# Loading 68 rows of one x block in sixteen 17-row transfers from GpSimd's queue

## The chip, the cores and the metric

One core of one Trainium2 chip. The metric is the time of one execution on the device, in microseconds (us), lower is better.

## The reference, cut to what matters

```python
# inputs (4096, 32, 64) f32, W (496, 64, 64) f32, out (4096, 496, 64) f32
idx_i, idx_j = np.triu_indices(32, k=1)          # 496 pairs i < j
vidots = jnp.einsum('bpd,pde->bpe', inputs[:, idx_i, :], W)
return vidots * inputs[:, idx_j, :]
```

The input is 33.5 MB, the weights 8.1 MB, and the output 520 MB: the kernel's work on memory is nearly all output.

## The kernel before

The 4,096 rows are 16 blocks of 256; a block holds two rows on each of 128 partitions and is computed in two passes of 46 steps. A pass `t` has five groups of steps, and each group fills one buffer `ot` and sends it out as one transfer of 2.9 to 3.4 MB. In a step TensorE multiplies into PSUM, then VectorE multiplies the result by x into `ot`; in seven steps of a pass ("aside") ACT copies PSUM to SBUF and GpSimd makes the product.

```python
xpool = ctx.enter_context(tc.tile_pool(name="xpool", bufs=2))   # x blocks
tpool = ctx.enter_context(tc.tile_pool(name="tpool", bufs=4))
opool = ctx.enter_context(tc.tile_pool(name="opool", bufs=3))   # outputs
# ... (cut)
def new_x(blk):
    xs[blk] = xpool.tile([P, 1 + NB * F, D], F32, tag="xs", name=f"xs_{blk}")
    nc.gpsimd.memset(xs[blk][:, 0, :], 0.0)

def load_x(blk, eng, k0=0, k1=NB):
    src = rows_of(x, blk).rearrange("(p k) f d -> p (k f) d", k=NB)
    eng.dma_start(out=xs[blk][:, 1 + k0 * F : 1 + k1 * F, :], in_=src[:, k0 * F : k1 * F, :])
# ... (cut)
LATE = 6
loads = {place[blk * NB, LATE]: blk + 1 for blk in range(2, NBLK - 1)}
# ... (cut) in the loop over the steps:
    if s in loads:
        new_x(loads[s])
        load_x(loads[s], nc.scalar)          # 128 rows of 16 KB, 2 MB
# ... (cut)
    if i in aside and c0 == 0 and s not in no_aside:
        nc.scalar.copy(tmp, src)
        nc.gpsimd.tensor_mul(dst, tmp, xj)
    else:
        nc.vector.tensor_mul(dst, src, xj)
    if pa + m in ends:
        nc.sync.dma_start(out=..., in_=ot[...])   # one output
```

## Time and profile before

| | before |
|---|---|
| time, median of 2 | 1354.19 us (1353.6 to 1354.78) |
| DMA engines, mean busy | 90% or more in 39 of 40 slices |
| TensorE / VectorE / GpSimd busy | 87% / 71% / 39% |
| output transfers | 161, 520 MB |
| loads of x by ACT's queue | 14 of 2 MB |

The prediction below shows the page's lines for this.

### The profile page before, as it was taken

The numbers are of one execution on the slowest core, as the hardware profiler recorded it, in microseconds if no ns is written. First come the engines' busy times: TensorE is split into PE (matmuls) and PEld (weight loads), VectorE is DVE, ScalarE is ACT, GpSimd is POOL, SyncE is SP. The second block draws the span as 40 slices with busy tenths as digits, with TensorE's granted clock in tenths as the row PEclk, the third lists the DMA queues.
The fourth block names the chain that finished last, engine by engine and source line by source line (L and its number), as shares of the span: only waits on it lengthen the run. The fifth ranks groups of instructions, "written<-read, shape, count | busy, mean of one in ns | idle before, by whom it ended". The sixth has DMA issues, their size and how long they took to land.

```text
span 1353.3 us, 17856 instructions
## 1 busy us (share of the span) xinstructions
PE 1180.3 (87%) x7424; PEld 690.9 (51%) x7424; DVE 956.9 (71%) x1262; ACT 374.1 (28%) x367; POOL 530.2 (39%) x246
## 2 busy tenths in 40 slices
PE   6989889889799897988879989888987989988994
PEld 4556545545455454555445545454554545545552
DVE  5778768767677676776757777676775767767774
ACT  3432222222232232222222222222222222223221
POOL 1813424444243443433444334433434434344431
PEclk9989999989999898999989999899998999989997
DMA  9999999999999999999999999999999999999997
GB/s 386 370 426 408 424 427 431 428 432 431 418 414 419 433 412 418 422 413 426 428 407 422 417 425 410 423 421 407 425 410 426 419 422 427 401 432 428 415 417 319
DMA packets 26273, 562.92 MB, mean 416 GB/s; under 512 B 2912, under 2 KB 2912, under 8 KB 3040
## 3 DMA queue, kind: packets, MB, share of 16 engines
q1 hardware_dynamic: 24048, 530.59, 92.4%
q10 hardware_dynamic: 2144, 31.20, 5.5%
q8 instruction: 58, 0.95, 0.3%
q14 instruction: 23, 0.19, 0.0%
HBM read 41.68 MB, written 520.09 MB: 415 GB/s over the span
## 4 chain that ended last, share of the span: by engine, by line
DMA 50%; PE 25%; DVE 17%; POOL 3%; issue 2%; ACT 0%; DVEq 0%; SPq 0%; POOLq 0%; ACTq 0%
DMA out_dram<-ot 50%; PE ps L211 20%; DVE ot L228 17%; PE ptx L114 4%; POOL ot L226 3%; PE ptw L104 1%; DMA raw<-in_L_rec_W_dram 1%; ACT tmp L225 0%; DVE rp L95 0%; POOL rp L95 0%; DVEq L228 0%; ACT wT L107 0%; SPq L76 0%; POOLq L226 0%; SPq L233 0%
## 5 line engine op out<-in xcount | busy, mean ns | idle before, releaser
L228 DVE TENSOR_TENSOR ot<-ps,xs 128x1024 f32<-128x1024 f32 (+15 forms) x1252 | 945.6, 808 | 364.7 <-DMA out_dram<-ot 185.9
L211 PE MATMUL ps<-wT,xT 64*128 64x512 f32 (+13 forms) x6272 | 1034.9, 473 | 132.8 <-DVE ot L228 121.3
L211 PEld LDWEIGHTS ps<-wT,xT 64*128 64x128 f32 x6272 | 563.7, 197 | 569.9 <-DVE ot L228 306.8
L226 POOL TENSOR_TENSOR ot<-tmp,xs 128x1024 f32<-128x1024 f32 x220 | 519.6, 2362 | 647.4 <-ACT tmp L225 457.1
L225 ACT COPY tmp<-ps 128x1024 f32<-128x1024 f32 x220 | 222.7, 1012 | 500.1 <-PE ps L211 459.6
L118 ACT COPY xT<-ptx 128x1024 f32<-128x1024 f32 x128 | 129.6, 1012 | 428.2 <-PE ptx L114 428.2
L114 PE MATMUL ptx<-ident,xs 128*128 128x128 f32 x1024 | 141.2, 281 | 18.5 <-DVE ot L228 9.9
L114 PEld LDWEIGHTS ptx<-ident,xs 128*128 128x128 f32 x1024 | 111.0, 142 | 64.3 <-issue 44.1
L72 POOL MEMSET xs<- 128x64 f32 x16 | 2.4, 152 | 148.6 <-DVE ot L228 148.6
L104 PE MATMUL ptw<-ident,rp 128*128 128x128 f32 (+1 forms) x128 | 19.2, 305 | 3.9 <-DVE rp L95 3.9
L104 PEld LDWEIGHTS ptw<-ident,rp 128*128 128x128 f32 (+1 forms) x128 | 16.2, 160 | 10.3 <-DVE rp L95 5.0
L107 ACT COPY wT<-ptw 128x1024 f32<-128x1024 f32 (+1 forms) x15 | 14.8, 984 | 21.4 <-PE ptw L104 21.4
L95 DVE COPY rp<-raw 128x1024 f32<-128x1024 f32 (+1 forms) x9 | 10.7, 1219 | 11.1 <-DMA raw<-in_L_rec_W_dram 11.1
L95 POOL COPY rp<-raw 128x1024 f32<-128x1024 f32 x4 | 8.0, 1994 | 0.1
L95 ACT COPY rp<-raw 112x1024 f32<-112x1024 f32 (+1 forms) x3 | 5.9, 1959 | 5.1 <-POOL ot L226 3.3
L107 DVE COPY wT<-ptw 128x1024 f32<-128x1024 f32 x1 | 1.2, 1224 | 3.3 <-PE ptw L104 3.3
L118 ACT ACT_TABLE_LOAD x1 | 1.3, 1283 | 0.7 <-PEq L251 0.7
masks.py:197 POOL MEMSET ident<- 128x128 f32 x1 | 0.2, 206 | 0.3 <-POOLq L251 0.3
masks.py:199 POOL TENSOR_SCALAR_AFFINE_SELECT ident<-ident 128x128 f32<-128x128 f32 x1 | 0.3, 295 | 0.0
L251 POOL MEMSET const-float32-0.0<- 128x1 f32 x1 | 0.1, 99 | 0.2 <-issue 0.2
L251 POOL MEMSET const-bfloat16-1.0<- 128x1 bf16 x1 | 0.1, 102 | 0.0
L251 POOL MEMSET const-uint8-127<- 128x1 uint8 x1 | 0.1, 102 | 0.0
(1 smaller groups left out, 0.1 us busy)
## 6 DMA issues: line engine op xcount, KB each, us to landing
out_dram<-ot SPq DMA_DIRECT2D x64, 3360.0 KB, 16.2
out_dram<-ot SPq DMA_DIRECT2D x32, 3168.0 KB, 15.4
out_dram<-ot SPq DMA_DIRECT2D x32, 3104.0 KB, 17.0
out_dram<-ot SPq DMA_DIRECT2D x31, 2880.0 KB, 16.4
xs<-in_r_inputs_dram ACTq DMA_DIRECT2D x14, 2048.0 KB, 16.6
raw<-in_L_rec_W_dram SPq DMA_DIRECT2D x3, 2048.0 KB, 14.3
xs<-in_r_inputs_dram SPq DMA_DIRECT2D x2, 1024.0 KB, 10.9
xs<-in_r_inputs_dram SPq DMA_DIRECT2D x1, 2048.0 KB, 24.6
```

Source lines behind the costliest of these rows:

```text
L72: nc.gpsimd.memset(xs[blk][:, 0, :], 0.0)
L95: copy(rp[:r], src[:, k * EU : (k + 1) * EU])
L104: nc.tensor.transpose(pt[:, n, :r], rp[:r, n].rearrange("p h d -> p (h d)"), ident[:r, :r])
L107: copy(wT[c][:, :, k * EU : (k + 1) * EU], pt[:, :, :r].rearrange("p e r -> p r e"))
L114: nc.tensor.transpose(pt[:, n, :], xs[blk][:, s : s + 2, :].rearrange("p f d -> p (f d)"), ident)
L118: copy(xT, pt)
L211: nc.tensor.matmul(ps[:, h, lo - pa : hi - pa, :], xT[blk, kt, n // RUN][h * D : (h + 1) * D, n % RUN, :], wT[c][h * D : (h + 1) * D, lo - ...
L225: nc.scalar.copy(tmp, src)
L226: nc.gpsimd.tensor_mul(dst, tmp, xj)
L228: nc.vector.tensor_mul(dst, src, xj)
L251: nc = _bacc.Bacc("TRN2", target_bir_lowering=False, num_devices=1)
```

## The change

The intent: take one x block of sixteen (block 7) mostly off ACT's queue and load it little by little from GpSimd's queue while block 6 is computed. 68 rows go in 16 pieces, four groups of 17 rows times four quarters of the 32 fields, written as one piece every fourth step; the other 60 rows stay with ACT's queue. The bytes are the same.

```diff
-    def load_x(blk: int, eng, k0: int = 0, k1: int = NB):
+    def load_x(blk: int, eng, k0: int = 0, k1: int = NB, r0: int = 0):
         src = rows_of(x, blk).rearrange("(p k) f d -> p (k f) d", k=NB)
-        eng.dma_start(out=xs[blk][:, 1 + k0 * F : 1 + k1 * F, :], in_=src[:, k0 * F : k1 * F, :])
+        eng.dma_start(
+            out=xs[blk][r0:, 1 + k0 * F : 1 + k1 * F, :], in_=src[r0:, k0 * F : k1 * F, :]
+        )
+    ODD, ODDR, ODDQ = 7, 17, 4
+
+    def load_piece(blk: int, n: int):
+        r, q = divmod(n, ODDQ)
+        rows = slice(r * ODDR, (r + 1) * ODDR)
+        cut = slice(q * F // ODDQ, (q + 1) * F // ODDQ)
+        src = rows_of(x, blk).rearrange("(p k) f d -> p k f d", k=NB)
+        dst = xs[blk][:, 1:, :].rearrange("p (k f) d -> p k f d", k=NB)
+        nc.gpsimd.dma_start(out=dst[rows, :, cut, :], in_=src[rows, :, cut, :])
 # ... (cut)
+    pieces = {place[(ODD - 1) * NB, LATE] + 4 * n + 1: n for n in range(ODDQ * ODDQ)}
 # ... (cut)
-            load_x(loads[s], nc.scalar)
+            load_x(loads[s], nc.scalar, r0=ODDR * ODDQ if loads[s] == ODD else 0)
+        if s in pieces:
+            load_piece(ODD, pieces[s])
```

## The prediction

The record as it stood before the result. What it took from no trace or run of this case is cut, and the cuts are marked. Its sum came to +7 us for the stall (5.5 + 1.5), and with the other outcomes weighed in to 1358.5 us. Terms of that sum are cut: what an issue on GpSimd takes, which the sums below still count as 1 us (an assumption then; the changed kernel's trace shows 0.972 us, mean of 16), and the time from an output's issue to its first byte, which is the step from 542.5 to 544.5 and from 552.5 to 554 (not shown before the result; 0.83 us measured in it). Cut, too, are the terms for how many bytes the late engine would be spared or given, which is why the hidden form has a range of 1350 to 1357.

> **What bounds the kernel now.** I read the page's rows by slice first, then the DMA queues, the groups, the waits, and the trace around the place where block 7 is loaded.
>
> ```profile
> DMA  9999999999999999999999999999999999999997
> ...
> DMA packets 26273, 562.92 MB, mean 416 GB/s; under 512 B 2912, under 2 KB 2912, under 8 KB 3040
> ...
> q1 hardware_dynamic: 24048, 530.59, 92.4%
> q10 hardware_dynamic: 2144, 31.20, 5.5%
> q8 instruction: 58, 0.95, 0.3%
> ...
> DMA 50%; PE 25%; DVE 17%; POOL 3%; issue 2%; ACT 0%; DVEq 0%; SPq 0%; POOLq 0%; ACTq 0%
> ...
> L228 DVE TENSOR_TENSOR ot<-ps,xs 128x1024 f32<-128x1024 f32 (+15 forms) x1252 | 945.6, 808 | 364.7 <-DMA out_dram<-ot 185.9
> ...
> out_dram<-ot SPq DMA_DIRECT2D x64, 3360.0 KB, 16.2
> ...
> xs<-in_r_inputs_dram ACTq DMA_DIRECT2D x14, 2048.0 KB, 16.6
> ```
>
> The DMA engines are at 90% or more in every slice but the last; no compute engine is. The chain that ended last is half DMA, all of it output. VectorE's largest idle time ends with the landing of an earlier output (three ot buffers). A 3,360 KB output needs 16.2 us to land though 16 engines move it in about 8: two outputs are normally queued.
>
> The trace's semaphore events show more. Each transfer ends with 16 increments, one per DMA engine. Times of issue, of the median engine and of the last one, around block 7's load, in us:
>
> ```
> output t=11 g=3   issued 505.39  median 514.89  last 523.23
> output t=11 g=4   issued 514.33  median 529.15  last 534.36
> x, block 7 (ACT)  issued 514.37  median 529.33  last 531.39
> output t=12 g=0   issued 520.65  median 535.97  last 541.35
> output t=12 g=1   issued 529.08  median 543.32  last 549.02
> output t=12 g=2   issued 541.76  median 550.88  last 556.84
> ```
>
> One engine ends 5 to 8 us after the others, at every output. At the kernel's end it moves packets until 1351.2 when the others stopped at 1345.0. A 26,880-byte packet takes 996 ns, so an average engine's 35.1 MB need 35.1/0.02699 = about 1,302 us; the late one has about 40 us more work. The 58 instruction packets (one per 22 us, 16 KB, 0.9 us each, some 50 us) are of that size; that they are its extra load is my inference. **The bound is the queue of this late engine**; the others have 3% to spare. It idles only if an output is issued later than its previous one ends: output g=0 of t=12 came at 520.65 and that engine could begin it at 534, so a delay under about 8 to 13 us is hidden.
>
> [...] during block 7's load one engine's packets run q10 16 KB, q1 26 KB, q10 16 KB, q1 26 KB and so on, singly, 8 of each; the load took 17.02 us for 2 MB.
> [...]
>
> **The change, part by part.**
> *Bytes.* The same 2 MB. 16,384 bytes take 611 ns and 8,192 take 309, so a packet costs 7 ns plus its bytes at 27.1 per ns, and 2 KB cost 83 ns. 16 pieces x 34 packets = 544 packets instead of 68 of 16 KB: 476 x 7 ns / 16 engines = 0.2 us. [...]
>
> *GpSimd's work.* [...]
>
> ```profile
> 514.42 0.15 POOL L72 MEMSET xs<- 128x64 f32 x1 [10.22 <-DVE ot L228]
> 517.82 2.36 POOL L226 TENSOR_TENSOR ot<-tmp,xs 128x1024 f32<-128x1024 f32 x1 [3.25 <-ACT tmp L225]
> 523.36 2.36 POOL L226 TENSOR_TENSOR ot<-tmp,xs 128x1024 f32<-128x1024 f32 x1 [3.18 <-DMA out_dram<-ot]
> 526.68 2.37 POOL L226 TENSOR_TENSOR ot<-tmp,xs 128x1024 f32<-128x1024 f32 x1 [0.96 <-ACT tmp L225]
> 534.49 2.35 POOL L226 TENSOR_TENSOR ot<-tmp,xs 128x1024 f32<-128x1024 f32 x1 [5.44 <-issue]
> 539.37 2.36 POOL L226 TENSOR_TENSOR ot<-tmp,xs 128x1024 f32<-128x1024 f32 x1 [2.53 <-ACT tmp L225]
> ```
>
> This is GpSimd in before, from the memset of block 7's buffer on. The instruction order of the built changed kernel is not one issue every fourth step: five pieces follow the memset directly, then the product that before ran at 517.82, two pieces, the product of 523.36, one piece, and then pieces 8, 9 and 10 ahead of the product of 526.68; 11, 12, 13 ahead of the next; 14 and 15 ahead of the one after. GpSimd's transfers share eight semaphores, so **piece n from 8 on waits in GpSimd's stream for piece n−8 to have landed**, with the products behind it. TensorE's and VectorE's order is unchanged; their new waits are for pieces needed from about 593 us on.
>
> *When piece 0 lands.* On one engine, taking turns with output packets, its 17 turns of 4 KB take 17 x (1.0 + 0.16) = 20 us; with 34 turns of 2 KB, 34 x 1.08 = 37 us. Issued at about 515.5, it lands at 537 in the first case. In the second it lands there too, since while GpSimd waits no output is issued, and an ordinary engine has no output left from about 534 on; the rest then passes at 83 ns a packet.
>
> *What that costs.* GpSimd would want to issue piece 8 at about 527 (five pieces to 519.6, product to 522, two pieces, product to 526.5, one piece). Waiting to 537, plus three issues and the product of 2.37 us, puts output t=12 g=1 at 542.5 instead of 529.08. The late engine ends t=12 g=0 at 541.35 − 2.4 us (64 KB of x not yet moved) = 539. [...] it idles 539 to 544.5: 5.5 us. Three more issues, a product, two issues, a product (3 + 2.4 + 2 + 2.4 = 10 us) put output g=2 at 552.5, at the engine about 554, where g=1 ends at 552.5: 1.5 us more. After that GpSimd has only products and catches up. Sum: **+7 us**, once, since only one of sixteen blocks is so loaded. Pieces 8 to 15 go out by 551 and have 40 us before use; no second stall.
>
> **Rivals.**
> *Hidden anyway.* If a piece is spread over nine engines (4 packets each, about 6 us to land), or its 34 descriptors go as one packet in one turn (about 3 us), piece 8 never waits. The issues then put output g=1 at 533 instead of 529, within the slack. Cost 0[...]. [...] Time 1350 to 1357.
> *All pieces on one engine.* [...] 544 packets x 83 ns = 45 us fall on one engine within a block, of which 8 to 14 us are hidden by queued outputs: +30 to +37 us, 1385 to 1392. [...] It is the main way to over 2%.
> *GpSimd becomes the bound.* If an issue costs 3 us instead of 1, five ahead of the first product delay output g=0 by 12 us, just about the slack, and the later ones add up: +10 to +15 us. [...]
>
> **Range and chances.** I give the 7 us stall one half, the hidden form (mean 0) 0.35, the expensive forms 0.15 (mean +22): 3.5 + 0 + 3.3 = about +6.8; the most likely single outcomes lie between 0 and +7, so I put it below the mean, at 1358.5. Range 1352 to 1371. Over 2% slower means above 1381: 0.07. Over 2% faster would need 27 us saved at an engine that keeps its bytes: 0.01. Within 2%: 0.92.
>
> **What would show it.** Right: an idle GpSimd of about 10 us ahead of a piece in block 6, ended by the landing of an earlier GpSimd load; output t=12 g=1 issued some 13 us later than before; a dip in the DMA row in one slice near 540 us; landings of pieces of 20 us and more; 544 packets of 2 KB; VectorE not waiting for x. Wrong if pieces land in under 10 us (the stall vanishes), if GpSimd's products lie far apart without a landing between them (the issue is dear), or if one engine's output lags by tens of us [...]. A change of VectorE's or TensorE's busy time is not expected.

## More of the kernel before

One more view serves for comparison: the view by windows, which gives for a stretch of time each engine's busy time (with the number of instructions), then the granted clock of TensorE, the share that the DMA engines were busy, and GB/s. This is the kernel before, in the stretch where the changed kernel will differ:

```profile
core 0: us, PE busy (x) PEld busy (x) DVE busy (x) ACT busy (x) POOL busy (x), PEclk, DMA share, GB/s
535.00:545.00 10.00, 9.70 (x58) 6.42 (x60) 6.61 (x11) 3.26 (x4) 6.57 (x3) 0.79 1.01 432
```

The last two figures are to be seen: the engines are full (1.01) and move 432 GB/s.

## The result

The changed kernel takes 1362.62 us (1362.52 to 1362.72, 2 runs) against 1354.19: 8.4 us more. Ratios here and below are the mean time of one kernel's fast runs over that of the other's of the same rounds, so not quite the ratio of the medians quoted; here 1.006, with a 95% interval of 1.0036 to 1.0084. That is within 2%, and inside the predicted range.

The page of the changed kernel: DMA share and GB/s by slice, packets, queues, and the group of GpSimd's new issues (busy time, mean ns of one, idle time before them and what ended it).

```profile
DMA  9999999999999997999999999999999999999997
GB/s 381 371 432 420 422 428 432 424 432 424 419 424 415 410 432 290 384 422 431 428 429 430 425 425 427 421 421 413 426 412 420 421 418 421 413 435 417 418 420 317
DMA packets 30813, 562.97 MB, mean 414 GB/s; under 512 B 7247, under 2 KB 7247, under 8 KB 7647
...
q0 software_dynamic: 4608, 1.15, 0.5%
...
L90 POOL DMA_DIRECT2D xs<-in_r_inputs_dram x16 | 15.5, 972 | 12.8 <-DMA xs<-in_r_inputs_dram 12.2
```

The DMA row now has one 7, in slice 16 (510 to 544 us), where GB/s fall to 290, and to 384 in the next. GpSimd waited 12.2 us ahead of its own issues, until an earlier load of x had landed. The new queue q0 carried 4,608 packets, though the 1.11 MB of x that it moves fill only 272 of 4 KB: the trace's packet records show 272 of 4,096 bytes, 256 of 4 (the increments) and **4,080 of 8 bytes**.

GpSimd's instructions in order of time (start, duration, instruction, count; in brackets the idle time before it and what ended it):

```profile
514.08 0.15 POOL L72 MEMSET xs<- 128x64 f32 x1 [10.37 <-DVE ot L245]
514.78 4.92 POOL L90 DMA_DIRECT2D xs<-in_r_inputs_dram  x5 [0.55 <-issue]
519.73 2.35 POOL L243 TENSOR_TENSOR ot<-tmp,xs 128x1024 f32<-128x1024 f32 x1
522.02 1.93 POOL L90 DMA_DIRECT2D xs<-in_r_inputs_dram  x2
524.05 2.34 POOL L243 TENSOR_TENSOR ot<-tmp,xs 128x1024 f32<-128x1024 f32 x1
526.35 0.98 POOL L90 DMA_DIRECT2D xs<-in_r_inputs_dram  x1
538.45 0.96 POOL L90 DMA_DIRECT2D xs<-in_r_inputs_dram  x1 [11.12 <-DMA xs<-in_r_inputs_dram]
540.51 1.91 POOL L90 DMA_DIRECT2D xs<-in_r_inputs_dram  x2 [1.10 <-DMA xs<-in_r_inputs_dram]
542.44 2.37 POOL L243 TENSOR_TENSOR ot<-tmp,xs 128x1024 f32<-128x1024 f32 x1
544.74 2.88 POOL L90 DMA_DIRECT2D xs<-in_r_inputs_dram  x3
```

Pieces 0 to 7 go out until 527.3. Piece 8 then waits 11.12 us for piece 0 to land, piece 9 waits again, and the product that ran at 526.68 before stands behind them until 542.44. The chain of waits of the changed kernel passes through just this:

```profile
515.88 24.34 DMA xs<-in_r_inputs_dram
...
540.51 1.91 POOL xs L90 x2
542.44 2.09 POOL ot L243
```

The stretch that was full before, by windows:

```profile
535.00:545.00 10.00, 8.48 (x61) 4.67 (x58) 6.15 (x10) 3.20 (x4) 5.43 (x5) 1.00 0.32 74
```

The DMA engines are busy 0.32 of it and move 74 GB/s instead of 432. The issues and last landings of the outputs, from the trace's semaphore events (us; last = the sixteenth increment):

```
                    before              after
                 issued   last      issued   last      last, later by
t=12 group 0     520.65  541.35     522.11  540.03       -1.3
t=12 group 1     529.08  549.02     544.84  555.97        7.0
t=12 group 2     541.76  556.84     554.27  567.81       11.0
t=12 group 3     549.42  565.11     558.87  575.79       10.7
t=13 group 3     587.88  606.49     598.17  615.37        8.9
```

Output group 1 is issued 15.8 us later. The late engine's last packet of group 0 ended at 539.47, and the first packets of group 1 are at 545.67: a hole of 6.2 us, in which, but for one packet of instructions, only pieces moved. Group 2 ends 11 us later than before; at the end of the program 7.4 us of that are left (spans 1360.7 and 1353.3 us).

### The profile page after: what moved, and what is told of

Its sections match the earlier page's. It is cut to its first block, busy times and chain, and to the rows that moved or that the text cites. A ratio compares the mean times of both kernels' runs of the same rounds, so it can differ in the third digit from the quotient of the medians.

```text
span 1360.7 us, 17892 instructions
## 1 busy us (share of the span) xinstructions
PE 1179.0 (87%) x7424; PEld 692.2 (51%) x7424; DVE 956.4 (70%) x1262; ACT 374.0 (27%) x367; POOL 544.7 (40%) x262
## 3 DMA queue, kind: packets, MB, share of 16 engines
q0 software_dynamic: 4608, 1.15, 0.5%
## 4 chain that ended last, share of the span: by engine, by line
DMA 48%; PE 26%; DVE 17%; POOL 5%; issue 3%; ACT 1%; DVEq 0%; SPq 0%; POOLq 0%; ACTq 0%
DMA out_dram<-ot 45%; PE ps L228 21%; DVE ot L245 17%; POOL ot L243 4%; PE ptx L128 4%; DMA xs<-in_r_inputs_dram 2%; PE ptw L118 1%; DMA raw<-in_L_rec_W_dram 1%; ACT tmp L242 1%; POOL xs L90 1%; DVE rp L109 0%; POOL rp L109 0%; DVEq L245 0%; ACT wT L121 0%; POOLq L243 0%
## 5 line engine op out<-in xcount | busy, mean ns | idle before, releaser
L90 POOL DMA_DIRECT2D xs<-in_r_inputs_dram x16 | 15.5, 972 | 12.8 <-DMA xs<-in_r_inputs_dram 12.2
## 6 DMA issues: line engine op xcount, KB each, us to landing
out_dram<-ot SPq DMA_DIRECT2D x32, 3168.0 KB, 15.5
```

Of the source, the lines that this page charges most:

```text
L90: nc.gpsimd.dma_start(out=dst[rows, :, cut, :], in_=src[rows, :, cut, :])
```

## The experiments

**The theory.** In the words used here, a ring is the packets that a queue has on one DMA engine, and a turn is one packet of a ring. That an engine alternates between two rings is seen in the kernel before: during block 7's load the packets of one engine are of q10 (16 KB, 611 ns) and of q1 (26 KB, 996 ns) in turn, 8 of each. A 17-row transfer from GpSimd's queue takes 17 turns in the ring of *every* DMA engine, 17 packets of 4 KB on one engine and 17 of 8 bytes on each of the other 15 (15 x 17 = 255 a piece, 16 pieces: 4,080, as counted). Beside queued outputs a turn lasts as long as an output packet, 0.86 to 1.0 us (medians of 855, 921 and 996 ns by size). So pieces land some 15 us after one another, or when outputs run out; piece 8 waits for that in GpSimd's stream; products wait behind it; an output is late; the engines go empty. **The rivals:** the issues' own time on GpSimd (15.5 us), the traffic of small packets on GpSimd's queue as such, and a fixed cost of having the queue in the program. The plain form of the theory, which the prediction had, says that a piece occupies one engine alone.

The trace of the changed kernel already speaks against the plain form. Eight pieces are issued by 527.3, but until 534.1 only twelve packets of 4 KB start, the first at 522.86, one at a time and 1.0 to 1.35 us apart (after one pair 0.16 us apart, at 527.65 and 527.81): the later pieces' data does not move while the first piece takes its turns. From then on up to seven such packets are under way at once, so the pieces do not all lie on one engine either.

The first four runs shared a chip and the runs of the kernel before (median 1355.1, 1354.24 to 1355.49, 7 runs).

### Sixteen rows instead of seventeen

```diff
-    ODD, ODDR, ODDQ = 7, 17, 4
+    ODD, ODDR, ODDQ = 7, 16, 4
```

> 16 rows a piece instead of 17 (64 rows left to ACT's queue); the same 16 issues, in the same places of GpSimd's stream, sharing the same eight semaphores. Theory (a 17-row piece takes 17 turns on every DMA engine, so it lands some 20 us after its issue or when the outputs run out, and piece 8 waits for that in GpSimd's stream ahead of a product): with 16 rows a piece is one turn on each engine, lands in 3 to 6 us, piece 8 does not wait, the output of pass 12 group 1 is issued at about 533 instead of 544.84, DMA stays full; time 1352 to 1357. Rival one (the 16 issues of 0.97 us ahead of the products are the cost): still about 1362. Rival two (small packets or uneven engines are the cost): the 256 packets of 4 KB stay, the 4,080 packets of 8 bytes should go; 1354 to 1358.

Measured: 1355.99 us (1355.85 to 1356.26, 4 runs), ratio 1.0007 (0.999 to 1.0024). The new queue now has 256 packets of 4 KB, 256 increments and no packet of 8 bytes. GpSimd around piece 8:

```profile
526.46 1.04 POOL L90 DMA_DIRECT2D xs<-in_r_inputs_dram  x2
529.37 0.50 POOL L90 DMA_DIRECT2D xs<-in_r_inputs_dram  x1 [1.86 <-DMA xs<-in_r_inputs_dram]
530.20 0.50 POOL L90 DMA_DIRECT2D xs<-in_r_inputs_dram  x1 [0.33 <-DMA xs<-in_r_inputs_dram]
530.72 2.35 POOL L243 TENSOR_TENSOR ot<-tmp,xs 128x1024 f32<-128x1024 f32 x1
```

Piece 8 goes out without a wait (second of the first line), 9 and 10 wait 2.2 us together, the product runs at 530.72, and the output of group 1 is issued at 533.10. One row fewer a piece removes the loss, with the same number of issues in the same places. The issues themselves became cheaper, though (0.5 us instead of 0.97), so this run alone does not clear them. A miss in the expectation: the pieces did not land in 3 to 6 us but in 11 to 17, some 2 us after one another, which fits pieces that stand behind one another in the same rings (two turns of 0.86 to 1.0 us each, by estimate one for the data and one for the increment; no run separates the two).

### Only eight pieces, so that none waits

```diff
-    pieces = {... for n in range(ODDQ * ODDQ)}
+    pieces = {... for n in range(2 * ODDQ)}        # rows 0 to 33
-            load_x(loads[s], nc.scalar, r0=...)
+            if loads[s] == ODD:                    # load_x with an end row r1
+                load_x(ODD, nc.scalar, r0=2 * ODDR, r1=2 * ODDR + 64)
+                load_x(ODD, nc.scalar, r0=2 * ODDR + 64)
```

> Only pieces 0 to 7, that is rows 0 to 33 in eight transfers of 17 rows; ACT's queue loads the other 94 rows as 64 and 30. No piece waits for a semaphore, so nothing holds GpSimd's products back. Theory in its full form (every piece takes 17 turns on all 16 engines, also on those that get only 8-byte packets): outputs of block 6 are issued on time (group 1 of pass 12 by about 532), but on the late engine 8 x 17 = 136 turns beside outputs of about 0.95 us each last until about 645, unless the outputs run out; TensorE and VectorE need the pieces from about 592 on, so they wait for x there 10 to 20 us and the loss comes back in block 7: 1359 to 1368. Theory in its plain form (only the wait in GpSimd's stream costs, a piece keeps one engine busy): landed by 555, time 1353 to 1356. Rival of issue cost: half of the loss, about 1358.

Measured: 1361.4 us (1361.07 to 1361.95, 4 runs), ratio 1.0047 (1.0032 to 1.0062). The products of block 6 are not held (group 1 is issued at 530.84), and the loss still comes, elsewhere. Last landings of the pieces, and a line of the timeline where TensorE first needs block 7:

```
piece      0      1      2      3      4      5      6      7
issued   514.3  515.4  516.4  517.3  518.3  521.5  522.5  523.5
last     541.5  556.7  570.3  585.2  603.4  605.7  605.9  606.1
```

```profile
603.77 1.94 PE L128 MATMUL ptx<-ident,xs 128*128 128x128 f32 x8 [10.60 <-DMA xs<-in_r_inputs_dram]
```

The first four pieces land 14 to 15 us after one another, about the time of 17 output packets, and piece 4 after 18.2 us; then the outputs run out and the last three land within half a microsecond. TensorE starts its transpose only when piece 4 is in, and from 595 to 605 the DMA engines are busy 0.40 of the time. This refutes the plain form (it expected no loss), and the issues' time (half of them, yet most of the loss).

### Two blocks loaded in this way

```diff
-    pieces = {place[(ODD - 1) * NB, LATE] + 4 * n + 1: n for n in ...}
+    pieces = {place[(b - 1) * NB, LATE] + 4 * n + 1: (b, n) for b in (ODD, 11) for n in ...}
```

> Block 11 is loaded in the same way as block 7. If the loss is a single stall per block so loaded, as theory has it, it comes twice: 1362.6 + 8.4 = 1371 (1368 to 1374), with a second dip of the DMA row some 330 us after the first. If it is a fixed cost of having the third queue in the program (start, end), the time stays at about 1362 to 1364.

Measured: 1369.65 us (1369.29 to 1370.2, 4 runs), ratio 1.0108 (1.0093 to 1.0123): 14.6 us over before, 7.3 a block. The page's DMA row of this kernel:

```profile
DMA  9999999999999997999999999799999999999997
```

A second 7, ten slices (340 us) after the first. The loss belongs to the load, not to the presence of the queue. The expectation was 1371, inside its range (1368 to 1374). Whether the second block costs a little less than the first is not shown: in this run GpSimd waited 11.6 us ahead of the issues of the first and 11.2 ahead of those of the second.

### All sixteen pieces, no products behind them

```diff
-        if i in aside and c0 == 0 and s not in no_aside:
+        if i in aside and c0 == 0 and s not in no_aside and t not in (12, 13):
```

> All 16 pieces, but block 6's 14 products that GpSimd made go to VectorE, so nothing stands behind the waiting pieces in GpSimd's stream. VectorE's work in passes 12 and 13 grows by 7 x 1.22 = 8.5 us each, to about 38 of 41 us. Plain form of the theory (products held back behind the wait are all of the loss): outputs of block 6 on time, 1353 to 1358. Full form (17 turns on every engine for each piece): outputs of block 6 on time, so the outputs never run out, and on the late engine pieces land about 16 us after one another: piece 12, which TensorE needs at about 592, is not even issued by then; TensorE and VectorE wait for x at the start of block 7 for 15 us or more; 1362 to 1378.

Measured: 1366.75 us (1366.25 to 1367.03, 4 runs), ratio 1.0086 (1.0071 to 1.0101): worse than the change itself. GpSimd has only issues in this stretch:

```profile
537.99 0.96 POOL L90 DMA_DIRECT2D xs<-in_r_inputs_dram  x1 [15.28 <-DMA xs<-in_r_inputs_dram]
553.33 0.96 POOL L90 DMA_DIRECT2D xs<-in_r_inputs_dram  x1 [14.38 <-DMA xs<-in_r_inputs_dram]
569.83 0.96 POOL L90 DMA_DIRECT2D xs<-in_r_inputs_dram  x1 [15.55 <-DMA xs<-in_r_inputs_dram]
584.70 0.96 POOL L90 DMA_DIRECT2D xs<-in_r_inputs_dram  x1 [13.92 <-DMA xs<-in_r_inputs_dram]
603.04 0.96 POOL L90 DMA_DIRECT2D xs<-in_r_inputs_dram  x1 [17.38 <-DMA xs<-in_r_inputs_dram]
```

Each of the pieces 8 to 12 waits 14 to 17 us for one earlier piece: the turns, undisturbed. Outputs of block 6 are on time to the last but one (587.28; before 587.88). Then TensorE waits for x, in its longest wait 16.3 us. Its stream has the first transposes of block 7 ahead of block 6's last four steps (`AHEAD = 4` in the kernel), so the last output of block 6 is issued at 613.25 instead of 596.64. So the stall of the changed kernel was probably in part a help: by stopping the outputs early it let the pieces through.

### Eighteen rows

A second chip, with the kernel before at 1354.63 (1354.2 to 1355.24, 7 runs).

```diff
-    ODD, ODDR, ODDQ = 7, 17, 4
+    ODD, ODDR, ODDQ = 7, 18, 4
```

> 18 rows a piece instead of 17 (56 rows left to ACT's queue): more bytes through GpSimd's queue, still 16 issues and the same waits on eight shared semaphores. [...] a piece is 2 turns on an engine and one for its increment, not 17. Theory by turns: pieces land about 3 us after one another, piece 8 waits little, the output of pass 12 group 1 is issued by about 537 and the late engine does not run out: 1353 to 1358. Rival (any number of rows that is no multiple of 16 is dear, or bytes on GpSimd's queue are dear): 1362 or more.

Measured: 1355.78 us (1355.63 to 1356.33, 4 runs), ratio 1.001 (0.9993 to 1.0026). More bytes than with 17 rows go through GpSimd's queue, and the loss is gone. The packet records show 288 of 4 KB and 224 of 8 bytes, that is 18 and 14 a piece: 9 engines x 2 and 7 engines x 2. Pieces land 2 to 3 us after one another, and GpSimd waits 7.0 us for them in five waits, none over 2.3. So it is neither the bytes nor a number of rows that is no multiple of 16; what is left of the causes named is the number of turns.

### Four pieces of seventeen rows

```diff
-    pieces = {... for n in range(2 * ODDQ)}        # from the run with eight
+    pieces = {... for n in range(ODDQ)}            # rows 0 to 16; ACT's queue: 96 and 15 rows
```

> Only pieces 0 to 3, rows 0 to 16, in four transfers of 17 rows; ACT's queue loads the other 111 rows as 96 and 15. No piece waits for a semaphore in GpSimd's stream. Theory by turns: 4 x 17 = 68 turns of about 0.95 us on the late engine, from 520 on, so all have landed by about 585 to 590, just ahead of their use at about 592 to 598: no loss, 1353 to 1357, with landings of 35 to 70 us in the trace. Eight pieces (136 turns) cost 6 us. Rival (each 17-row piece costs about 0.8 us wherever it lands): 1357 to 1358.

Measured: 1354.61 us (1353.88 to 1355.01, 4 runs), ratio 0.9999 (0.9984 to 1.0014). The four land last at 541.7, 556.9, 571.4 and 586.3, again 15 us apart, all before 592. The long landings are all there, 27 to 69 us, and cost nothing, because nothing waits for them. With eight, four pieces landed after that (603.4 to 606.1), and the loss was 6.3 us.

### Which engine ends last

The prediction's first step says that one engine bounds the kernel. A probe of it, with loads of x cut so that some may use fewer than 16 engines, one run of a kernel that is no candidate (1391.95 us, state unknown; its time is not used). The edit, in the kernel before:

```diff
+    SPLIT = {4: (104, 24), 6: (88, 40), 8: (81, 27, 18, 2),
+             10: (119, 7, 2), 12: (115, 5, 5, 3), 14: (123, 3, 2)}
-            load_x(loads[s], nc.scalar)
+            load_split(loads[s], nc.scalar)        # the rows in transfers of these sizes
```

> A probe of which DMA engine ends last, not a candidate. The kernel before, with the x loads of blocks 4, 6, 8, 10, 12 and 14 split by rows [...] (104+24, 88+40, 81+27+18+2, 119+7+2, 115+5+5+3, 123+3+2 rows). [...] If the late engine is not among those used, its lag behind the median shrinks in that block (it moves no x there, the others more); if it is among them, it ends still later, alone behind the others of its group. Time 1360 to 1410, of no importance.

The increments of these loads come as 14, 12, 10, 8, 6 and 4 events: one at about 0.5 us after the issue, then 13, 11, 9, 7, 5 and 3 more. They are read here as one for all unused engines together and one for each engine used. Landings of outputs queued beside two of the loads, in us from issue, sorted by engine:

```
5 engines used (block 12), output issued 942.3:
  9.3 9.3 9.3 9.3 9.4 9.4 9.4 10.1 10.2 10.8 11.0 | 17.0 17.0 17.0 17.1 | 23.4
3 engines used (block 14), output issued 1132.8:
  8.7 8.7 8.8 8.8 8.8 8.8 8.8 8.9 8.9 9.4 9.9 11.2 | 15.3 | 26.0 26.1 26.1
```

With five engines used, four are late together and one, later still, completes their number; with three used, three are late together and one lies alone between them and the rest. So the late engine is, by this reading, among the five and not among the three. Which one it is is not shown: the traces carry no engine numbers. In the kernel before, from 300 us on, every output's last increment comes 3 us or more after its fifteenth; what makes that engine late is not shown.

No experiment points to a version that beats the kernel before: the harmless forms only reach its time.

## Why the prediction was right, and where its steps were not

- **The bound.** Held: every loss here is a time in which outputs were issued too late for the late engine. "At every output" was too much: in before the last increment is 0.1 to 2.4 us behind the median at the outputs issued up to 200 us, and over 5 us behind at every output only from 300 us on (once before, 6.0 us at 256), so the lag builds up. The inference that the instruction packets are its extra load finds no support: in the run with none of block 6's products on GpSimd all engines are within 1.3 us of one another after the stall, and from there the late one falls behind by 0.2 to 0.4 us at most outputs, between 797 and 848 us with no step at the instruction packets, which come every 22 us. The cause stays open.
- **Bytes and packets.** 544 packets of 2 KB were expected; there were 272 of 4 KB (160 ns each) and 4,080 of 8 bytes (9 ns). As traffic that is as small as thought: q0 has 0.5% of the engines' time. As turns it is the cause.
- **GpSimd's issues.** 1 us was right (0.972), but by luck: no trace had shown it, and the same 16 issues take 0.52 us each with 16 rows and 0.60 with 18. From the first issue to the first packet on q0 it was 6.6 us here (514.78 to 521.41), with outputs queued; piece 8, with an output left on one engine alone, had its first increment after 2.1 us.
- **When piece 0 lands.** 537 was predicted, 538.16 measured. The mechanism, turns that alternate with output packets until the outputs run out, held (packets of 4 KB 1.0 to 1.35 us apart until 534). What failed is the thought that a piece keeps one engine and leaves the others free: the median engine, too, posted piece 0's increment only at 534.97. For piece 0 this changes nothing; for pieces behind it everything, as the run with eight showed.
- **Output group 1.** 542.5 predicted, 544.84 measured: piece 9 waited once more (1.10 us), and piece 8 left 1.4 us later.
- **The holes.** 5.5 us predicted for the first, 6.2 measured, with two errors against each other: the output came 2.3 us later than predicted, but its first packet 0.83 us after the issue, sooner than the term that is cut had it. The second hole, 1.5 us, did not come on the last engine, whose packets of group 1 end and of group 2 begin at 555.31. By output group 2 the prediction had 7.0 lost, the landings show 11.0. This is the mis-sized term: in before all of block 7 had been moved by 531.4, while after the stall pieces 11 to 15 still shared the rings with groups 1 and 2 (an engine that carries one takes an estimated 17 x 0.16 = 2.7 us for it). Some 3.6 us were regained by the end: the late engine, no longer so far behind the others (1.7 us behind the median at the outputs issued at 642 to 664 us, 5.7 again at 805), lost less ground than in before for some outputs.
- **No second stall.** Held, but barely. The prediction gave pieces 8 to 15, all issued by 551, 40 us before their use. Piece 15, issued at 550.92, took 55.7 us and landed at 606.65, since the late engine took 17 turns for each of the last three pieces (576.78, 591.61, 606.65), and VectorE began block 7 at 607.45; in before it began it at 597.38. So the first stall had moved the need back by 10 us, and the 40 us would not have been enough.
- **The rivals.** The hidden form was given 0.35 and did not happen here; rows16 and rows18 are what it looks like. Pieces on one engine only, and dear issues, did not happen. The central number, 1358.5, averaged these; the branch that came true said +7, and +8.4 was measured. VectorE's and TensorE's busy time did not change (956.9 and 956.4 us; 1180.3 and 1179.0), as stated.

What stays open besides the late engine: no run takes the semaphore wait away while the products stay behind the same 16 pieces, since the program shares eight semaphores; what the wait costs alone is read from the trace, not from an experiment.

## What to carry to other kernels

Count a small transfer from GpSimd's queue not by its bytes but by its turns: the packets that it puts on one engine (by the packet counts here 17 of 17 rows, 2 of 18, 1 of 16), times the length of the packets it alternates with (0.86 to 1.0 us here). A row count of 16, or 18, instead of 17 made the difference between 1 or 2 turns and 17, and with full rings between 2 us and 15 us per transfer. And look at what stands behind a transfer in its engine's stream: from the ninth piece on it was a wait, and the products that completed an output stood behind it; the same long landings cost nothing where (four pieces) nobody needed them yet.
